# Quarter turn on the raw indices, one mask for sines and cosines, two standing index tiles

## The chip, the cores and the metric

The kernel runs on one core of a Trainium2 chip. The metric is device time in microseconds (us) of one execution, as the median of several runs. Five engines work side by side, each through its own instructions in order: TensorE (PE) multiplies matrices, VectorE (DVE) and ScalarE (ACT) do elementwise work, GpSimd (POOL) some small elementwise work, and SyncE (SP) issues all the transfers. An instruction that depends on another engine's result waits on a semaphore, and everything behind it on its own engine waits with it.

## The reference, cut to what matters

Audio of 32 rows is cut into 313 frames of 512 samples each, turned by a cosine transform, and passed through one attention layer and one feed-forward layer. The change touches only the feed-forward layer:

```python
wavelength = 1.0 + jnp.abs(W)                      # W is [256, 512]
theta = x[..., None, :] / wavelength + B_param     # x is [32, 313, 512], normalised
idx = jnp.mod(jnp.round(theta * (4096 / TWO_PI)), 4096).astype(jnp.int32)
sin_theta, cos_theta = sin_t[idx], cos_t[idx]      # tables of 4096 entries
cos_sum = jnp.sum(cos_theta * attn_cos, axis=-1)   # over the 512 features
sin_sum = jnp.sum(sin_theta * attn_sin, axis=-1)
out = einsum(cos_sum, proj_cos_w) + einsum(sin_sum, proj_sin_w)
return jax.nn.silu(out)
```

For each of 32 x 313 frames, 256 units and 512 features one index, one sine and one cosine are formed: 1.28 thousand million of each. The sums over the features are matrix products.

## The kernel before, in words

**Layout.** The 512 features lie on the 128 partitions in 4 chunks (`NC4`), the 313 frames of a sequence (`S`) along the free dimension. `xT` holds the normalised input of up to eight sequences, as a ring of four pairs. `f` holds, for each unit and feature, a factor and an offset, so that one VectorE instruction with an int16 output makes the rounded table index of one unit.

**Rounds and slots.** The 256 units are taken in 8 blocks of 32. A round (`ffn_round`, L566) does one block for all sequences that are in the ring; a pair joins at the round that `STARTS` gives and stays for eight rounds. The work of a round is cut into slots. A slot holds up to 16 (`SLOT`) stretches of 313 elements: `r` sequences times `n_p` combinations of unit and chunk. With two, four or eight sequences in the ring that is 5008 elements per partition, with six it is 3756.

**One slot before.** The steps are, with the lines of the profile:

1. L610 (`index`), VectorE: indices of the slot from `xT` and `f`, float32 to int16, in one instruction for every run of neighbouring pairs. It fills a new tile `ix`.
2. L622 (`mask`), VectorE: that tile in place, and 4095, exclusive or 2048. The second operation shifts the angle by half a turn, so that the sine's argument lies between -pi and pi.
3. L643 (`sines`), ScalarE: the sines of the tile, into a tile `trig`.
4. L630 (`quarter`), VectorE: the masked tile plus 1024 (a quarter turn), into a second tile `ix`.
5. L636 (`wrap`), VectorE: that second tile in place, and 4095.
6. L643 again, ScalarE: the sines of the second tile, which are the cosines.
7. L664 (`go`), TensorE: after each of the two activations, 16 (or 12) matrix products of `trig` with `hot`, which add into the PSUM banks `pa`.

In the code, the loop `for k in (1, 0)` goes through steps 1 to 3 with `k = 1` and through 4 to 6 with `k = 0`. There are four buffers `ix` (`N_IX`), so two slots' worth, and three buffers `trig`. A new tile of `ix` has to wait until the readers of the tile that lay in the buffer before it are done.

At the end of a round the banks are copied out (L681) and stored.

**What sets the order.** Nothing is issued as the code is walked through. Every step is added to a plan (`Plan`, with a key, an engine, an assumed duration, what it reads and what it writes). `Plan.emit` then plays the engines forward in time with these assumed durations and always takes, on each engine, the ready step with the lowest key. The order so found is the order of the instructions on each engine. The feed-forward rounds and the attention of later sequences (`attention`, with keys spread over the time that it may take) are thus woven into each other: attention's VectorE, ScalarE and TensorE instructions stand between those of the slots.

`swap` (L779) closes the buffers of the second sequence's attention and opens the pools in which `ix`, `trig`, `hot` and `f` lie. It comes before the first round.

Of the kernel before, what the change touches and what calls it, by code (L numbers as in the profile page):

```python
# [14 lines left out]
I16 = mybir.dt.int16  # L15
# [111 lines left out]
def tile_audio_tower(ctx: ExitStack, tc: tile.TileContext, t: dict, out: bass.AP):  # L127
# [5 lines left out]
    ROW0 = [i * STEP for i in range(NT)]  # L133
    NB = 4
    N_RING = 3
    N_IX, N_TRIG, N_HOT, N_PA = 4, 3, 2, 4

    const = ctx.enter_context(tc.tile_pool(name="const", bufs=1))
    psum = ctx.enter_context(tc.tile_pool(name="psum", bufs=1, space=PSUM))
# [426 lines left out]
    def ffn_round(plan, k0, blk, ring):  # L566

        pairs = [(at, pair) for at, pair in enumerate(ring) if pair is not None]  # L570
        r = 2 * len(pairs)
        runs = []
        for j, (at, _) in enumerate(pairs):
            if runs and runs[-1][0] + runs[-1][2] == at:
                runs[-1][2] += 1
            else:
                runs.append([at, j, 1])
        n_p = min(SLOT // r, 2 * NC4) if SLOT % r == 0 else 2
        E = n_p * r * S
        n_slots = 2 * NC4 // n_p  # L580
        n_banks = -(-r // 4)
        fz = place("f", 2)
        plan.add(k0 - 8, "SP", DMA_NS,
                 lambda: nc.sync.dma_start(
                     new("f", fz, [P, 2, NC4, UNITS], bufs=2), f_d[blk]),
                 ("f_d",), (("f", fz),))
        banks = {}
        key = k0
        for n in range(0, UNITS, 2):
            z = place("hot", N_HOT)  # L590
            plan.add(key - 4, "SP", DMA_NS,
                     lambda n=n, z=z: nc.sync.dma_start(
                         new("hot", z, [P, 2, NC4, 2, 32], bufs=N_HOT),
                         t["hot"][:, blk * UNITS + n : blk * UNITS + n + 2]),
                     (), (("hot", z),))
            todo = [(c, u) for c in range(NC4) for u in range(2)]
            for i in range(n_slots):
                parts = todo[i * n_p : (i + 1) * n_p]
                xs = None
                for k in (1, 0):  # L600
                    x = place("ix", N_IX)
                    if k == 1:
                        for pt, (c, u) in enumerate(parts):
                            for at, j, m in runs:
                                def index(x=x, pt=pt, c=c, u=u, n=n, at=at, j=j, m=m):
                                    if pt == 0 and j == 0:
                                        new("ix", x, [P, SLOT * S], I16, bufs=N_IX)
                                    d0 = (pt * r + 2 * j) * S
                                    f = now["f", fz]
                                    nc.vector.tensor_scalar(  # L610
                                        now["ix", x][:, d0 : d0 + 2 * m * S],
                                        now["xT", c][:, 2 * at * S : 2 * (at + m) * S],
                                        f[:, 0, c, n + u : n + u + 1], f[:, 1, c, n + u : n + u + 1],
                                        ALU.mult, ALU.add)
                                plan.add(key, "DVE", 233 + 0.521 * 2 * m * S, index,
                                         (("f", fz), *(("xT", c, at + y) for y in range(m))),
                                         (("ix", x),))


                        def mask(x=x):  # L620
                            tl = now["ix", x][:, :E]
                            nc.vector.tensor_scalar(  # L622
                                tl, tl, LUT - 1, LUT // 2, ALU.bitwise_and, ALU.bitwise_xor)
                        plan.add(key, "DVE", 130 + 0.26 * E, mask, (), (("ix", x),))
                        xs = x
                    else:

                        def quarter(x=x, xs=xs):
                            tl = new("ix", x, [P, SLOT * S], I16, bufs=N_IX)
                            nc.vector.tensor_scalar(  # L630
                                tl[:, :E], now["ix", xs][:, :E], float(LUT // 4), None, ALU.add)
                        plan.add(key, "DVE", 160 + 0.26 * E, quarter, (("ix", xs),), (("ix", x),))

                        def wrap(x=x):
                            tl = now["ix", x][:, :E]
                            nc.vector.tensor_scalar(tl, tl, LUT - 1, None, ALU.bitwise_and)  # L636
                        plan.add(key, "DVE", 130 + 0.26 * E, wrap, (), (("ix", x),))

                    w = place("trig", N_TRIG)

                    def sines(x=x, w=w):
                        tl = new("trig", w, [P, SLOT * S], bufs=N_TRIG)
                        nc.scalar.activation(tl[:, :E], now["ix", x][:, :E], AF.Sin,  # L643
                                             bias=-PI32, scale=ANG)
                    plan.add(key, "ACT", 110 + 0.8333 * E, sines, (("ix", x),), (("trig", w),))

                    first = n == 0 and i == 0
                    if first:  # L650
                        banks[k] = [place("pa", N_PA) for _ in range(n_banks)]

                    def go(k=k, n=n, w=w, z=z, parts=parts, first=first):
                        if first:
                            for p in banks[k]:
                                new("pa", p, [P, 512], bufs=N_PA, pool="bank")
                        for c in dict.fromkeys(c for c, _ in parts):
                            for bk, p in enumerate(banks[k]):
                                alone = r - 4 * bk == 2
                                for pt, (c_, u) in enumerate(parts):  # L660
                                    for b in range(min(4, r - 4 * bk) if c_ == c else 0):
                                        g = b + 2 * u if alone else b
                                        s0 = (pt * r + 4 * bk + b) * S
                                        nc.tensor.matmul(  # L664
                                            now["pa", p][g * 32 : g * 32 + 32, :S],
                                            now["hot", z][:, u, c, k, :],
                                            now["trig", w][:, s0 : s0 + S],
                                            start=(n == 0 and c == 0 and (alone or u == 0)),
                                            stop=(n == UNITS - 2 and c == NC4 - 1
                                                  and (alone or u == 1)),  # L670
                                        )
                    plan.add(key, "PE", 169 * n_p * r, go, (("trig", w), ("hot", z)),
                             [("pa", p) for p in banks[k]])
                    key += n_p * r / SLOT
                    if n < UNITS - 2 or i < n_slots - 1:
                        continue
                    m, r0 = blk * UNITS // P, blk * UNITS % P
                    for bk, p in enumerate(banks[k]):
                        u = place("part", 2)
                        plan.add(key, "DVE", 490,  # L680
                                 lambda u=u, p=p: nc.vector.tensor_copy(  # L681
                                     new("part", u, [P, S], bufs=2), now["pa", p][:, :S]),
                                 (("pa", p),), (("part", u),))
                        alone = r - 4 * bk == 2
                        for b in range(min(4, r - 4 * bk)):
                            sq = 2 * pairs[2 * bk + b // 2][1] + b % 2

                            which = [(b, 0, 1)] if not alone else [(b, 0, 2), (b + 2, 1, 2)]
                            for g, o, st in which:
                                plan.add(  # L690
                                    key, "SP", DMA_NS,
                                    lambda k=k, u=u, sq=sq, g=g, o=o, st=st: nc.sync.dma_start(
                                        sums_d[m, r0 + o : r0 + 32 : st, k, sq * S : (sq + 1) * S],
                                        now["part", u][g * 32 + o : g * 32 + 32 : st, :]),
                                    (("part", u),), (("sums_d", sq),),
                                )


    def load(key, *shape):
# [82 lines left out]
        pools["bank"] = ctx.enter_context(tc.tile_pool(name="bank", bufs=1, space=PSUM))  # L782
        for c in range(NC4):
            new("xT", c, [P, RING * S], bufs=NC4)
    plan.add(-9.0, "SP", 1, swap, (), [
        *plan.named("b"), *(("xT", c, at) for c in range(NC4) for at in range(RING // 2)),
        *(("hot", z) for z in range(N_HOT)), *(("f", z) for z in range(2))])


    life = NF // UNITS  # L790
# [10 lines left out]
                ring[at] = p  # L801
                joins[rd].append((p, at))
        rings.append(list(ring))
        key_of.append(key_of[-1] + 32.0 * sum(p is not None for p in ring))


    times, p, k = [], 1, 0.0
# [146 lines left out]
```

## Time and profile before

| | |
|---|---|
| median of 3 runs | 18893.47 us (18890.79 to 18904.49) |
| the profiled execution | 18894.1 us |
| its span | 18892.3 us |
| VectorE busy | 17770.2 us |
| ScalarE busy | 18090.3 us |
| TensorE matmul busy | 14803.3 us |
| mean granted TensorE clock | 0.926 |
| index (L610) | 5888 instructions, 6673.8 us |
| mask (L622), quarter (L630), wrap (L636) | 2144 each; 3023.7, 3014.4, 3017.3 us |
| sines (L643) | 4288 activations, 17547.6 us |

How to read it: the profile is of one execution. Busy time is time in which an engine worked on an instruction; where two instructions of an engine overlap, the time counts once. A group is all instructions of one line, operation and tile. What ended an engine's idle time is inferred from the semaphores. The page also cuts the span into 40 slices and gives each engine's busy share in tenths (9 is 90% or more); one slice is 472 us.

### The profile page before, as it was taken

What the parts mean: (1) busy time and instruction counts of PE and PEld (TensorE: products, weight loads), DVE (VectorE), ACT (ScalarE), POOL (GpSimd) and SP (SyncE); (2) the same over time, 40 slices, a digit from 0 to 9 for tenths busy, and PEclk for the clock granted to TensorE, in tenths of its full rate; (3) what the DMA queues carried; (4) which work ended last, traced back from release to release, by engine and by line L of the source; (5) the groups of instructions that cost most, each with busy time, mean ns of one, the idle gap of its engine ahead of it and who ended that gap; (6) DMA issues with size and microseconds to landing.
All of it is one profiled execution on the core that took longest, in us unless ns stands there. A gap on an engine that the chain in (4) does not pass through costs nothing.

```text
span 18892.3 us, 332980 instructions
## 1 busy us (share of the span) xinstructions
PE 14803.3 (78%) x148864; PEld 6590.0 (35%) x148864; DVE 17770.2 (94%) x15244; ACT 18090.3 (96%) x5026; POOL 656.5 (3%) x1222
## 2 busy tenths in 40 slices
PE   8888888887888887888788888887888788766566
PEld 4433333333333333333333333333333333222222
DVE  5999999999999999999999999999999999889998
ACT  3899999999999999999999999999999999999998
POOL 0000000000000000000000000000000000000000
PEclk8999999999999999999999999999999999889998
DMA  3211111111111111111111111111111111000011
GB/s 96 66 52 48 50 57 47 46 51 47 31 35 37 46 42 41 32 40 46 38 45 39 32 44 41 45 40 36 39 38 46 39 45 35 24 10 25 12 30 46
DMA packets 447834, 783.69 MB, mean 41 GB/s; under 512 B 61601, under 2 KB 116129, under 8 KB 446401
## 3 DMA queue, kind: packets, MB, share of 16 engines
q1 hardware_dynamic: 446400, 762.39, 13.3%
q8 instruction: 1167, 19.12, 0.4%
q14 instruction: 267, 2.18, 0.0%
HBM read 657.51 MB, written 104.66 MB: 40 GB/s over the span
## 4 chain that ended last, share of the span: by engine, by line
DVE 55%; ACT 18%; PE 15%; issue 8%; POOL 3%; DMA 1%; DVEq 0%; SPq 0%; ACTq 0%; POOLq 0%
DVE ix L610 20%; ACT trig L643 18%; DVE ix L630 9%; DVE ix L622 9%; PE pa L664 8%; DVE ix L636 8%; PE a_W L288 3%; PE a_W L273 2%; DVE a_mx L363 1%; DVE a_prob L372 1%; DVE a_sm L397 1%; DVE a_probT L424 1%; DVE a_st L236 1%; PE a_W L355 1%; POOL a_lu L224 1%
## 5 line engine op out<-in xcount | busy, mean ns | idle before, releaser
L643 ACT ACTIVATE trig<-ix 128x5008 f32<-128x5008 int16 (+1 forms) x4288 | 17547.6, 4178 | 442.0 <-PE pa L664 185.5
L664 PE MATMUL pa<-trig,hot 128*32 128x313 f32 x131072 | 10373.1, 462 | 3021.0 <-ACT trig L643 3003.0
L664 PEld LDWEIGHTS pa<-trig,hot 128*32 128x32 f32 x131072 | 4058.5, 116 | 8907.0 <-ACT trig L643 4513.9
L610 DVE TENSOR_SCALAR ix<-xT,f 128x2504 int16<-128x2504 f32 (+3 forms) x5888 | 6673.8, 1184 | 211.9 <-ACT trig L643 205.8
L630 DVE TENSOR_SCALAR ix<-ix 128x5008 int16<-128x5008 int16 (+1 forms) x2144 | 3014.4, 1406 | 201.2 <-DVE ix L622 5.0
L622 DVE TENSOR_SCALAR ix<-ix 128x5008 int16<-128x5008 int16 (+1 forms) x2144 | 3023.7, 1410 | 69.2
L636 DVE TENSOR_SCALAR ix<-ix 128x5008 int16<-128x5008 int16 (+1 forms) x2144 | 3017.3, 1407 | 67.2
L288 PE MATMUL a_W<-a_xnT,a_ring 128*128 128x313 f32 x4960 | 1539.2, 446 | 220.1 <-DVE a_u L341 125.1
L273 PE MATMUL a_W<-a_ring,a_u 128*105 128x512 f32 x2256 | 1101.5, 623 | 120.8 <-DVE a_u L499 53.7
L288 PEld LDWEIGHTS a_W<-a_xnT,a_ring 128*128 128x128 f32 x4960 | 882.9, 191 | 868.2 <-issue 284.7
L430 PE MATMUL a_W<-a_h,a_probT 105*105 105x64 f32 x4464 | 540.6, 270 | 118.0 <-DVE a_probT L424 117.7
L273 PEld LDWEIGHTS a_W<-a_ring,a_u 128*105 128x105 f32 x2256 | 360.2, 174 | 722.8 <-issue 579.0
L430 PEld LDWEIGHTS a_W<-a_h,a_probT 105*105 105x105 f32 x4464 | 476.3, 181 | 386.4 <-issue 194.7
L355 PE MATMUL a_W<-a_u 64*105 64x313 f32 x1488 | 502.8, 466 | 112.0 <-DVE a_prob L372 100.6
L412 PE MATMUL a_W<-ident,a_prob 105*105 105x105 f32 x2232 | 325.9, 284 | 186.7 <-ACT a_prob L384 150.9
L273 PE MATMUL a_W<-a_ring,a_xnT 128*105 128x512 f32 x744 | 380.0, 631 | 50.9 <-DVE a_xnT L210 49.3
L224 POOL TENSOR_TENSOR a_gu<-a_gr 105x24 f32<-105x24 f32 x93 | 69.5, 747 | 10066.3 <-DVE a_gr L218 10061.4
L412 PEld LDWEIGHTS a_W<-ident,a_prob 105*105 105x105 f32 x2232 | 259.4, 185 | 344.9 <-ACT a_prob L384 193.2
L260 PE MATMUL a_W<-ident,a_xn 105*128 105x105 f32 x1116 | 190.2, 298 | 234.8 <-DVE a_xn L248 108.2
L355 PEld LDWEIGHTS a_W<-a_u 64*105 64x105 f32 x1488 | 239.3, 178 | 386.0 <-DVE a_prob L372 152.6
L363 DVE TENSOR_REDUCE a_mx<-a_W 105x3 f32<-105x939 f32 x248 | 280.2, 1130 | 17.7 <-PE a_W L355 17.1
L424 DVE TENSOR_TENSOR a_probT<-a_W,a_dec 105x939 f32<-105x939 f32 x248 | 279.9, 1129 | 13.0 <-PE a_W L412 13.0
(136 smaller groups left out, 3461.9 us busy)
## 6 DMA issues: line engine op xcount, KB each, us to landing
hot<-in_hot SPq DMA_DIRECT2D x672, 256.0 KB
a_dec<-in_decay SPq DMA_DIRECT2D x248, 260.5 KB
a_ring<-in_proj SPq DMA_DIRECT2D x128, 256.0 KB
a_ring<-in_dct SPq DMA_DIRECT2D x124, 256.0 KB
a_ring<-wv_d SPq DMA_DIRECT2D x124, 256.0 KB
a_ring<-in_wq SPq DMA_DIRECT2D x124, 256.0 KB
a_ring<-in_wk SPq DMA_DIRECT2D x124, 256.0 KB
a_ring<-in_wq_s SPq DMA_DIRECT2D x124, 256.0 KB
```

Of the source, the lines that this page charges most:

```text
L273: lambda c=c, i=i, k=k, to=to: nc.tensor.matmul(x.W[:N, to, :], lhsT[:, c, ROW0[i] : ROW0[i] + N], x.ring[k], start=(c == 0), stop=(c == N ...
L288: lambda c=c: nc.tensor.matmul(x.W[:, bank, :S], w[:, c, :], x.xnT[:, c, :], start=(c == 0), stop=(c == NC4 - 1)),
L355: lambda i=i, qk=qk, r0=r0: nc.tensor.matmul(x.W[:N, i, :S], qk[r0 : r0 + DH, 0, ROW0[i] : ROW0[i] + N], qk[r0 : r0 + DH, 1, :], start=Tru ...
L363: lambda m=m: nc.vector.tensor_reduce(m[:N], x.W[:N, :NT, :S], AX.X, ALU.max),
L412: nc.tensor.transpose(x.W[:N, jj, ROW0[i] : ROW0[i] + N], x.prob[:N, a, i, ROW0[j] : ROW0[j] + N], ident[:N, :N],)
L430: nc.tensor.matmul(x.y[:N, i, (hd % 2) * DH : (hd % 2 + 1) * DH], x.probT[:N, jj, ROW0[i] : ROW0[i] + N], x.v[:N, jj, hd * DH : (hd + 1) * ...
L610: nc.vector.tensor_scalar(now["ix", x][:, d0 : d0 + 2 * m * S], now["xT", c][:, 2 * at * S : 2 * (at + m) * S], f[:, 0, c, n + u : n + u + ...
L622: nc.vector.tensor_scalar(tl, tl, LUT - 1, LUT // 2, ALU.bitwise_and, ALU.bitwise_xor)
L630: nc.vector.tensor_scalar(tl[:, :E], now["ix", xs][:, :E], float(LUT // 4), None, ALU.add)
L636: nc.vector.tensor_scalar(tl, tl, LUT - 1, None, ALU.bitwise_and)
L643: nc.scalar.activation(tl[:, :E], now["ix", x][:, :E], AF.Sin, bias=-PI32, scale=ANG)
L664: nc.tensor.matmul(now["pa", p][g * 32 : g * 32 + 32, :S], now["hot", z][:, u, c, k, :], now["trig", w][:, s0 : s0 + S], start=(n == 0 and ...
```

## The change

- A slot has one tile `ix` with two halves, in place of two tiles. The quarter turn (L619) is added to the raw indices of half 0 and goes into half 1; then one instruction (L624) masks both halves, with the and and the exclusive or that only the first tile had before. The separate wrap is gone.
- The first activation of a slot (L632) reads half 0 and the second half 1. Both read what the one mask has written.
- The tiles `ix` are no longer made anew in each slot: two of them (`N_IX` is 2) are made in `swap` and stay for the whole kernel.
- In the plan, quarter and mask have the key of the slot's first half; their assumed durations are set anew.
- The slots are made from one list over the round's units and chunks, in the same order as before, and `hot` is fetched at the first slot that needs it.

```diff
-    N_IX, N_TRIG, N_HOT, N_PA = 4, 3, 2, 4
+    N_IX, N_TRIG, N_HOT, N_PA = 2, 3, 2, 4
...
-        n_p = min(SLOT // r, 2 * NC4) if SLOT % r == 0 else 2
-        E = n_p * r * S
-        n_slots = 2 * NC4 // n_p
+        n_p = SLOT // r
...
+        todo = [(n + u, c) for n in range(0, UNITS, 2) for c in range(NC4) for u in range(2)]
+        slots = [todo[i : i + n_p] for i in range(0, len(todo), n_p)]
...
-                for k in (1, 0):
-                    x = place("ix", N_IX)
...
-                                    if pt == 0 and j == 0:
-                                        new("ix", x, [P, SLOT * S], I16, bufs=N_IX)
...
-                        def mask(x=x):
-                            tl = now["ix", x][:, :E]
-                            nc.vector.tensor_scalar(
-                                tl, tl, LUT - 1, LUT // 2, ALU.bitwise_and, ALU.bitwise_xor)
-                        plan.add(key, "DVE", 130 + 0.26 * E, mask, (), (("ix", x),))
...
-                        def quarter(x=x, xs=xs):
-                            tl = new("ix", x, [P, SLOT * S], I16, bufs=N_IX)
-                            nc.vector.tensor_scalar(
-                                tl[:, :E], now["ix", xs][:, :E], float(LUT // 4), None, ALU.add)
-                        plan.add(key, "DVE", 160 + 0.26 * E, quarter, (("ix", xs),), (("ix", x),))
-
-                        def wrap(x=x):
-                            tl = now["ix", x][:, :E]
-                            nc.vector.tensor_scalar(tl, tl, LUT - 1, None, ALU.bitwise_and)
-                        plan.add(key, "DVE", 130 + 0.26 * E, wrap, (), (("ix", x),))
...
+            x = place("ix", N_IX)
...
+                            now["ix", x][:, 0, d0 : d0 + 2 * m * S],
...
+            def quarter(x=x, E=E):
+                tl = now["ix", x]
+                nc.vector.tensor_scalar(tl[:, 1, :E], tl[:, 0, :E], float(LUT // 4), None, ALU.add)
+            plan.add(key, "DVE", 220 + 0.26 * E, quarter, (("ix", x, 0),), (("ix", x, 1),))
+
+            def mask(x=x, E=E):
+                tl = now["ix", x][:, :, :E]
+                nc.vector.tensor_scalar(
+                    tl, tl, LUT - 1, LUT // 2, ALU.bitwise_and, ALU.bitwise_xor)
+            plan.add(key, "DVE", 220 + 0.26 * 2 * E, mask, (), [("ix", x, i) for i in range(2)])
+            for k in (1, 0):
...
+                    nc.scalar.activation(tl[:, :E], now["ix", x][:, 1 - k, :E], AF.Sin,
+                                         bias=-PI32, scale=ANG)
+                plan.add(key, "ACT", 110 + 0.8333 * E, sines, (("ix", x, 1 - k),), (("trig", w),))
...
+        for x in range(N_IX):
+            new("ix", x, [P, 2, SLOT * S], I16, bufs=N_IX)
...
-        key_of.append(key_of[-1] + 32.0 * sum(p is not None for p in ring))
+        key_of.append(key_of[-1] + 512.0 / SLOT * sum(p is not None for p in ring))
```

## The prediction

> **What bounds the kernel now.** I read the page first: the busy totals, the forty slices, the chain that ended last.
>
> ```profile
> PE 14803.3 (78%) x148864; PEld 6590.0 (35%) x148864; DVE 17770.2 (94%) x15244; ACT 18090.3 (96%) x5026; POOL 656.5 (3%) x1222
> DVE  5999999999999999999999999999999999889998
> ACT  3899999999999999999999999999999999999998
> DVE 55%; ACT 18%; PE 15%; issue 8%; POOL 3%; DMA 1%; DVEq 0%; SPq 0%; ACTq 0%; POOLq 0%
> ```
>
> Two engines are full together. ScalarE (ACT) has 18892.3 - 18090.3 = 802 us without work in the whole span, so no saving on VectorE (DVE) can be worth more than that, while the chain runs mostly through VectorE. An average cannot settle which one sets the pace, so I cut the span into stages.
>
> ```profile
> core 0: us, PE busy (x) PEld busy (x) DVE busy (x) ACT busy (x) POOL busy (x), PEclk, DMA share, GB/s
> 325.00:1500.00 1175.00, 947.83 (x8906) 463.08 (x8907) 1108.91 (x1312) 1053.93 (x408) 62.72 (x126) 0.91 0.20 60
> 1500.00:3200.00 1700.00, 1392.90 (x13468) 650.30 (x13470) 1636.58 (x1555) 1589.42 (x443) 64.35 (x115) 0.93 0.16 50
> 3200.00:5000.00 1800.00, 1449.30 (x14204) 649.32 (x14200) 1715.45 (x1564) 1689.34 (x539) 78.82 (x152) 0.95 0.15 45
> 5000.00:15000.00 10000.00, 8067.52 (x81709) 3577.59 (x81698) 9563.56 (x7248) 9888.60 (x2531) 397.25 (x684) 0.93 0.13 40
> 16400.00:18500.00 2100.00, 1308.75 (x15640) 495.27 (x15632) 1960.45 (x1993) 2087.02 (x554) 0.00 (x0) 0.92 0.06 19
> ```
>
> The columns are the stretch, its length, then busy time by engine. From 325 to 5000 ACT lacks 121 + 111 + 111 = 343 us (7%); from 5000 to 18500 it lacks about 1%. So there are two regimes. After 5000 ScalarE is the bound: 111 us idle in 10000. Before 5000 something holds it up. The chain of waits (total us, times, longest), first for 1000 to 3000 us, then for the whole span, names it:
>
> ```profile
> ACT trig L643 <- DVE ix L622: 63.5, 48, 4.1
> ACT trig L643 <- PE pa L664: 35.2, 18, 5.2
> ACT trig L643 <- DVE ix L636: 24.2, 14, 2.8
> ```
>
> ```profile
> DVE ix L610 <- ACT trig L643: 205.8, 264, 2.7
> ```
>
> Early, the sines wait for the index tiles (L622, L636), while VectorE waits for ScalarE (L610, index tile not free) in that stretch for 2.9 us only; most of the 205.8 us lies late. VectorE is the early bound. One slot at the full ring in the timeline, the groups of one line by shape, and ScalarE's timeline near the end:
>
> ```profile
> 10017.78 3.07 DVE L610 TENSOR_SCALAR ix<-xT,f 128x2504 int16<-128x2504 f32 x2
> 10020.88 1.47 DVE L622 TENSOR_SCALAR ix<-ix 128x5008 int16<-128x5008 int16 x1
> 10022.45 1.47 DVE L630 TENSOR_SCALAR ix<-ix 128x5008 int16<-128x5008 int16 x1
> 10023.95 1.47 DVE L636 TENSOR_SCALAR ix<-ix 128x5008 int16<-128x5008 int16 x1
> 10025.34 3.07 DVE L610 TENSOR_SCALAR ix<-xT,f 128x2504 int16<-128x2504 f32 x2
> ```
>
> ```profile
> L636 DVE TENSOR_SCALAR ix<-ix 128x5008 int16<-128x5008 int16 x1760 | 2578.2, 1465 | 55.4
> L636 DVE TENSOR_SCALAR ix<-ix 128x3756 int16<-128x3756 int16 x384 | 439.1, 1143 | 11.8
> ```
>
> ```profile
> 18698.37 150.01 ACT L643 ACTIVATE trig<-ix 128x5008 f32<-128x5008 int16 x35
> ```
>
> From start to start a VectorE slot takes 3.10 + 1.57 + 1.50 + 1.39 = 7.56 us; ScalarE's two sines take 2 x 150.01 / 35 = 8.57 us. Attention's VectorE work is put between: 2041 us (17770 less the four groups' 15,729), nearly all of it before 16400.
>
> **What the Trainium skill says.** "VectorE: DVE Perf Modes", in "The TRN2 errata", has a fixed cost per SBUF instruction, measured near 150 cycles, beside the cost per element. The trace agrees: (1465 - 1143) / (5008 - 3756) = 0.257 ns per element, leaving 177 ns fixed. The same page, in "What auto-detection actually checks", gives 16-bit one-source operations in SBUF four elements a cycle when the outermost count is even or equal; 0.257 ns is that rate at the page's 0.96 GHz, but no row of before has two separate rows. "ScalarE: Activation LUTs", in "What ACT_TABLE_LOAD costs", says that back-to-back activations overlap by about 93 ns; here each sine shows 4365 ns and the next starts 4286 ns after it, 79 ns of overlap.
>
> **The change part by part.**
>
> Removed: two masks a slot (L622 and L636, 2144 each), together 6041 us of busy time. Added: one mask over both halves. Its estimate: 1465 + 5008 x 0.257 = 2754 ns, and 1143 + 3756 x 0.257 = 2110 ns for the six-sequence rounds. 1760 x 2.754 + 384 x 2.110 = 5657 us. Busy time falls by 384 us, 0.18 us a slot. The quarter add stays one instruction of the same size. With the gaps: after is index 3.10, quarter 1.50 to 1.57, mask 1.39 + 1.29 = 2.68, so 7.28 to 7.35 us against 7.56. I take 0.21 us a slot (end 0.28); at 3756 elements the starts (1.25, 1.18, 1.05) give the same. 2144 x 0.21 = 450 us of VectorE's time, 2.5%.
>
> What of it counts: from 325 to 5000 there are 1101 sines, 550 slots: 550 x 0.21 = 116 us, if VectorE alone sets the pace. It doesn't wholly. ScalarE also waits there for TensorE (PE), 128 us in all, when matmuls on trig stand behind attention's matmuls, and VectorE itself waits for POOL and PE for some 110 us, both of which stay as long. I take 70%: 80 us; ends 40 and 116. From 5000 to 18500 the saving falls behind ScalarE, which covers it: 13500 us hold about 1550 slots, 326 us of saved work, but ScalarE's waits for index tiles there are only 30 us and for TensorE 57. I take 15 us; ends -60 and +80. If ScalarE's cover were gone it would be 326.
>
> Moved: the first sine. Before, it waited for index and mask, 3.10 + 1.47 = 4.6 us of a slot; in the built order of the changed kernel both sines stand behind the one mask, after the quarter add. Buffer reuse is unchanged: index waits for the first sine of two slots earlier, the quarter add for the second, in both kernels, so the standing tiles hold the same two slots as the four old tiles. From the time that the index tile is free, three sines of 4.29 (12.86 us) go by before the first sine is needed. Before, 4.6 us of VectorE's work had to fit in, leaving 8.3 us for attention's instructions; now 3.10 + 1.5 + 2.75 = 7.4 us, leaving 5.5. The waiting sine holds back only what is behind it on ScalarE, then the matmuls on TensorE, and attention's matmuls queued behind those. In the orders of both programs, the slots that hold more than 5.5 us of attention (instructions by their rows' means) are 17 before and 5 after of 2144, and those over 4 us 105 and 95. So I cost it at nothing where VectorE has its lead, and at the -60 end where it has not. At the start, once: first sine at 331.0, now 3 us later, in a stretch where VectorE is the bound, so hidden.
>
> Edits with one answer, nothing: the slot list, `key_of` and the loads of hot (same sizes: SLOT is 16 and divides as before); no DMA, no matmul and no activation is added. The last 150 us are one unbroken run of sines.
>
> Sum against the profiled execution (18894.1 us, span 18892.3, 0.6 us above the median of 18893.47): 18894 - 80 - 15 = 18799. I predict 18800 us.
>
> **The rivals.**
>
> *ScalarE is the bound throughout* (13%). For: 96% busy. Against: 7% idle before 5000, and the waits on L622. Then the early saving turns into longer waits of L610 for the sines and of ACT for PE: 10 to 35 us gained, about 18875.
>
> *The late stage gives too* (14%). ScalarE's remaining waits after 5000, 87 us, come partly from attention work late on VectorE; if two thirds go (58) and the early stage gives all 116: about 18715.
>
> *The first sine comes too late* (13%, the other side). Place: score phases after 5000, where two instructions of 1.13 to 1.15 us per head (L363, L372) fall into successive slots. A slot then takes 7.35 + 2.3 = 9.65 us against 8.57 and VectorE loses 1.1 us of its lead per slot, so a full lead of 5.5 us lasts five such slots; before, 1.3 us from 8.3, over six slots. It decides where more than five follow one another or the lead was not full. Of the attention passes, 20 come after 5000 us; at 7 us lost in each it is 140 us: 18894 - 80 + 140 = 18954. It cancels the early gain at 4 us a pass. Against: the late waits on L622 were 2.5 us in all, and 0.21 us more lead is won per slot.
>
> *The mask does not keep its rate* (4%) when its halves are not adjacent, which is so for the 384 slots of 3756 elements (at 5008 the built program has one run of 10016). At half the rate: 384 x 7512 x 0.257 ns = 740 us more, two thirds of it early where VectorE is the bound: 18894 - 80 + 493, about 19300. The change then would not do what it says.
>
> **How the numbers follow.** The likeliest case (56%): 18740 to 18856, at 18800. About 0.2% (38 us) is what a measurement of this kernel can tell from no change. Faster: 56 + 14 = 70%. Same: 13%. Slower: 13 + 4 = 17%. The range 18685 to 18920 takes in the first three cases but for the ends, and leaves out the 17% above and some 3% below.
>
> **What would show it.** The mask's group near 2754 and 2110 ns, x2144; the quarter add still 1465; VectorE's busy time near 17390; ScalarE's busy time unchanged at 18090 (each step's sizes). ScalarE's idle time from the start to the end of the early rounds down by 40 to 116 us, in waits for L622's successor; later, the index instructions waiting for sines well over 205.8 us in all, which is where the covered saving goes. Wrong if ScalarE's waits for the mask after 5000 exceed 100 us (first sine too late), if the two-row mask takes over 3 us, or if the saved early time comes back as waits for TensorE.

## The result and the profile after

The changed kernel takes 18832.92 us (median of 7 runs, 18820.34 to 18839.53) against 18896.91 us (7 runs): a ratio of 0.9965, 95% interval 0.9954 to 0.9977. That is 64 us saved where 94 were forecast, and inside the range. The profiled execution took 18838.41 us, its span 18836.6.

From the page of the kernel after, the busy totals and the chain that ended last by engine:

```profile
PE 14740.8 (78%) x148864; PEld 6575.9 (35%) x148864; DVE 17450.4 (93%) x13100; ACT 18081.3 (96%) x5026; POOL 722.1 (4%) x1222
ACT 31%; DVE 30%; PE 24%; issue 11%; POOL 3%; DMA 1%; SPq 0%; ACTq 0%; DVEq 0%; POOLq 0%
```

VectorE has 2144 instructions fewer and is busy for 320 us less (384 were forecast); ScalarE does the same work. The chain, 55% VectorE before, is now shared out. The groups by shape (count, busy us, mean ns, idle before, its releaser):

```profile
L624 DVE TENSOR_SCALAR ix<-ix 128x10016 int16<-128x10016 int16 x1760 | 4872.8, 2769 | 54.6
L619 DVE TENSOR_SCALAR ix<-ix 128x5008 int16<-128x5008 int16 x1760 | 2579.2, 1465 | 576.9 <-ACT trig L632 472.4 <-DVE ix L607 1.8
L624 DVE TENSOR_SCALAR ix<-ix 128x7512 int16<-128x7512 int16 x384 | 814.1, 2120 | 11.8
```

The mask is at its price: 2769 and 2120 ns, where 2754 and 2110 had been worked out. So the two halves that do not touch, in the 384 slots of 3756 elements, keep the rate of one run, as the Trainium skill has it for an even outermost count ("VectorE: DVE Perf Modes", "What auto-detection actually checks"). Unlooked-for is the second line: the quarter add waits for ScalarE, 472 us in this shape.

One slot in the timeline, start first:

```profile
10014.72 3.07 DVE L607 TENSOR_SCALAR ix<-xT,f 128x2504 int16<-128x2504 f32 x2
10017.89 1.47 DVE L619 TENSOR_SCALAR ix<-ix 128x5008 int16<-128x5008 int16 x1
10019.39 2.77 DVE L624 TENSOR_SCALAR ix<-ix 128x10016 int16<-128x10016 int16 x1
10022.08 1.13 DVE L424 TENSOR_TENSOR a_probT<-a_W,a_dec 105x939 f32<-105x939 f32 x1
```

From start to start that is 3.17 + 1.50 + 2.69 = 7.36 us, against 7.56 before: 0.20 us a slot. Over the whole traces, the slots of 5008 elements with no wait and no other work between have the same medians, 7.36 and 7.56. Over 2144 slots it is 429 us of VectorE's time, of which 64 arrived. The same stages as before (stretch, length, busy time by engine):

```profile
325.00:1500.00 1175.00, 948.50 (x8908) 462.89 (x8908) 1094.91 (x1202) 1052.18 (x408) 69.44 (x126) 0.91 0.20 60
1500.00:3200.00 1700.00, 1385.21 (x13613) 650.70 (x13615) 1626.67 (x1381) 1607.03 (x449) 76.90 (x128) 0.94 0.17 50
3200.00:5000.00 1800.00, 1455.51 (x14348) 656.75 (x14341) 1702.65 (x1329) 1710.48 (x548) 84.56 (x139) 0.95 0.15 45
5000.00:15000.00 10000.00, 8058.80 (x81850) 3578.86 (x81846) 9411.48 (x6129) 9893.63 (x2527) 435.92 (x684) 0.94 0.13 40
```

ScalarE's idle time from 325 to 5000 us fell from 342 to 305 us, 37 us; from 5000 to 15000 it fell by 5, after 15000 by 5 again, and its work is 9 us shorter. That makes the 56 us between the two spans. So early only about half of what was forecast came. The early waits of ScalarE are not those that I had named. From 325 to 5000 us (total us, times, longest), first before, then after:

```profile
ACT trig L643 <- PE pa L664: 127.7, 52, 6.1
ACT trig L643 <- DVE ix L622: 123.2, 78, 8.8
ACT trig L643 <- DVE ix L636: 42.2, 23, 2.8
ACT trig L643 <- issue: 37.2, 12, 6.2
```

```profile
ACT trig L632 <- DVE ix L624: 168.4, 78, 11.6
ACT trig L632 <- PE pa L654: 119.5, 64, 6.7
ACT trig L632 <- issue: 4.4, 1, 4.4
```

The waits for masks, which were to fall, went from 165 to 168 us. The gain lies in the waits for TensorE, which were to stay (8 us less), and in those marked "issue", for which the profile shows no releaser (33 us less); what those waited for stays open. Over the whole run, first before, then after:

```profile
ACT trig L643 <- DVE ix L622: 126.8, 89, 8.8
...
ACT trig L643 <- DVE ix L636: 69.6, 50, 2.8
```

```profile
DVE ix L619 <- ACT trig L632: 541.8, 684, 3.5
...
ACT trig L632 <- DVE ix L624: 253.5, 130, 11.6
...
ACT trig L632 <- PE pa L654: 138.1, 85, 6.7
```

Before, ScalarE waited 126.8 + 69.6 = 196 us for masks and wraps; now 254 us for the mask, though VectorE does less. From 5000 to 18500 us these waits rose from 30 to 84 us, while those for TensorE fell from 57 to 16. VectorE and ScalarE each wait for the other more than before: a sign that what lies ready between them has become less.

### The profile page after: what moved, and what is told of

Read it like the earlier page. It is cut to its first block, busy times and chain, and to the rows that moved or that the text cites. A ratio compares the mean times of both kernels' runs of the same rounds, so it can differ in the third digit from the quotient of the medians.

```text
span 18836.6 us, 330714 instructions
## 1 busy us (share of the span) xinstructions
PE 14740.8 (78%) x148864; PEld 6575.9 (35%) x148864; DVE 17450.4 (93%) x13100; ACT 18081.3 (96%) x5026; POOL 722.1 (4%) x1222
## 4 chain that ended last, share of the span: by engine, by line
ACT 31%; DVE 30%; PE 24%; issue 11%; POOL 3%; DMA 1%; SPq 0%; ACTq 0%; DVEq 0%; POOLq 0%
ACT trig L632 30%; PE pa L654 16%; DVE ix L607 10%; DVE ix L624 9%; DVE ix L619 5%; PE a_W L288 3%; PE a_W L273 3%; DVE a_mx L363 1%; POOL a_lu L225 1%; POOL a_lu L224 1%; PE a_W L355 1%; DVE a_prob L372 1%; POOL a_lu L226 0%; ACT a_prob L384 0%; DVE a_st L236 0%
## 5 line engine op out<-in xcount | busy, mean ns | idle before, releaser
L632 ACT ACTIVATE trig<-ix 128x5008 f32<-128x5008 int16 (+1 forms) x4288 | 17538.8, 4178 | 401.5 <-DVE ix L624 253.5
L624 DVE TENSOR_SCALAR ix<-ix 128x10016 int16<-128x10016 int16 (+1 forms) x2144 | 5686.9, 2652 | 66.4
L619 DVE TENSOR_SCALAR ix<-ix 128x5008 int16<-128x5008 int16 (+1 forms) x2144 | 3017.5, 1407 | 667.8 <-ACT trig L632 541.8
L224 POOL TENSOR_TENSOR a_lu<-a_lr 105x3 f32<-105x3 f32 x186 | 106.4, 572 | 4072.8 <-DVE a_lr L218 4063.1
```

The lines of the kernel that those rows point to most:

```text
L224: nc.gpsimd.tensor_tensor(u, r, r, ALU.mult)
L619: nc.vector.tensor_scalar(tl[:, 1, :E], tl[:, 0, :E], float(LUT // 4), None, ALU.add)
L624: nc.vector.tensor_scalar(tl, tl, LUT - 1, LUT // 2, ALU.bitwise_and, ALU.bitwise_xor)
L632: nc.scalar.activation(tl[:, :E], now["ix", x][:, 1 - k, :E], AF.Sin, bias=-PI32, scale=ANG)
```

## The lead, worked out again

"Lead" here is the time that VectorE may spend on attention's work in one slot before ScalarE runs dry, when it is as far ahead as the tiles let it be. In the built order the index of a slot waits for the first sine of two slots earlier, the quarter add for the second sine of two slots earlier. Before, that second wait came after index and mask, 4.6 us into the slot, when the second sine (4.29 us) was over. Now it comes after the index alone, at 3.2 us, so a VectorE that is fully ahead stands still until 4.29. The mask then ends at 4.29 + 1.50 + 2.77 = 8.6 us and the first sine is due at 12.9: a lead of 4.3 us, not 5.5. Before it was 8.3.

*Theory 1*: the time is set by VectorE's slot and by this lead together; the change earns with the first and pays with the second. *Theory 2*: the lead costs nothing; the rest of the gain is held up by TensorE's waits and attention's chains. Two further questions: what in the change shortens the slot, and how much of the 64 us is chance in the order of instructions, since each kernel gets its own from the planner. All times below are also given as a difference to the kernel before, measured beside each; the intervals on these ratios reach some 25 us to either side.

## Experiments

**Two masks again, half 1 first** (`split_late`).

```diff
-            def mask(x=x, E=E):
-                tl = now["ix", x][:, :, :E]
+            for h in (1, 0):
+                def mask(x=x, E=E, h=h):
+                    tl = now["ix", x][:, h, :E]
...
+                plan.add(key, "DVE", 110 + 0.26 * E, mask, (("ix", x, 1),) if h == 0 else (), [("ix", x, h)])
...
-                plan.add(key, "ACT", 110 + 0.8333 * E, sines, (("ix", x, 1 - k),), (("trig", w),))
+                plan.add(key, "ACT", 110 + 0.8333 * E, sines, [("ix", x, i) for i in range(2)], (("trig", w),))
```

> Standing tiles and the quarter turn on raw indices as in the change, but two masks again, half 1 first and half 0 last, so both sines still wait for the whole slot. VectorE has four instructions a slot as before the change (7.56 us). Theory 1, the change pays for its shorter VectorE slot with a smaller lead of the first sine (4.3 us instead of 8.3): slower than before, 18920 to 18990 us, ScalarE's waits for masks over 300 us. Theory 2, the lead costs nothing and only VectorE's instruction counts: within 20 us of before, 18880 to 18915.

Measured: 19166.71 us, +269 us, ratio 1.0142 (1.0128 to 1.0155). That is more than theory 1 had, and the test was not clean: with the last line the planner takes half 0 as in use until the second sine, and puts attention's VectorE work ahead of the index: counted in the traces, some 1710 us of it stand right behind a mask and 290 us behind an index, where `split_early` (next) has some 1030 and 990. ScalarE waits 601 us for masks. So the run mixes the lead with another order and doesn't decide between the theories; it shows only how much the order around the index can cost.

**The same, half 0 first** (`split_early`): `for h in (0, 1)`, without the two added conditions in the plan.

> The same with half 0 masked first, so that the first sine needs one mask fewer. VectorE's work as in split_late. Theory 1: 20 to 60 us faster than split_late, about 18900 to 18940. Theory 2: the same as split_late within 15 us.

Measured: 18838.88 us, -58 us, ratio 0.9969 (0.9958 to 0.9981): as fast as the change, with the same number of instructions a slot as before it. This I had not expected. The timeline of `split_early`:

```profile
10010.46 3.07 DVE L607 TENSOR_SCALAR ix<-xT,f 128x2504 int16<-128x2504 f32 x2
10013.70 1.47 DVE L619 TENSOR_SCALAR ix<-ix 128x5008 int16<-128x5008 int16 x1 [0.17 <-ACT trig L633]
10015.20 2.84 DVE L625 TENSOR_SCALAR ix<-ix 128x5008 int16<-128x5008 int16 x2
10017.96 3.08 DVE L607 TENSOR_SCALAR ix<-xT,f 128x2504 int16<-128x2504 f32 x2
```

The two masks take 2.84 us together although each shows 1.47: the second starts 1.37 us after the first. From the first to the next slot's index it is 2.76 us, against 2.69 with the one mask. So merging the masks saves 0.07 us a slot. The other 0.13 us come from the raw quarter turn: before, each of mask, quarter and wrap waited for the instruction in front of it (quarter and wrap started 1.57 and 1.50 us after it); now the quarter add and the first mask do, and the second mask waits for neither. VectorE's busy time bears it out: 17565.9 us here against 17770.2 with the same number of instructions, the overlap of the pair (0.10 us a slot).

**The clean version of the late order** (`split_late2`): `split_early` with half 1 masked first, and a token in the plan that keeps the two sines in their order and does nothing else.

```diff
-            for h in (0, 1):
+            for h in (1, 0):
...
-                plan.add(key, "DVE", 110 + 0.26 * E, mask, (), [("ix", x, h)])
+                plan.add(key, "DVE", 110 + 0.26 * E, mask, (("ix", x, 1),) if h == 0 else (),
+                         [("ix", x, h)] + ([("masked", x)] if h == 0 else []))
...
-                plan.add(key, "ACT", 110 + 0.8333 * E, sines, (("ix", x, 1 - k),), (("trig", w),))
+                plan.add(key, "ACT", 110 + 0.8333 * E, sines, (("ix", x, 1 - k), ("masked", x)), (("trig", w),))
```

> As split_early but half 1 masked first, with the planner told of nothing else than that both sines come after the mask of half 0 (in split_late it was also told that half 0 stays in use until the second sine, which moved attention's work). VectorE's slot 7.43 us as in split_early, the lead of the first sine 12.9 - 4.3 - 4.3 = 4.3 us instead of 5.6. Theory 1, the lead prices the change: 20 to 100 us slower than split_early, 18860 to 18940. Theory 2, it does not, and split_late was slow through the order alone: within 15 us of split_early, 18825 to 18855.

Measured: 18896.26 us, -5 us, ratio 0.9998 (0.9990 to 1.0007). VectorE is busy for 17565.7 us, as in `split_early` to 0.2 us, and attention's work stands much as it stood (some 1080 us behind masks, 990 behind indices). The first sine is released one mask later, 1.4 us, and the run is 53 us longer. In ScalarE's busy time, 15 us of the loss lie before 5000 us and 35 between 5000 and 15000. In the waits, first `split_early`, then `split_late2`:

```profile
DVE ix L619 <- ACT trig L633: 459.5, 607, 3.5
...
ACT trig L633 <- DVE ix L625: 211.3, 147, 10.3
...
ACT trig L633 <- issue: 40.0, 17, 4.5
```

```profile
ACT trig L634 <- DVE ix L625: 314.3, 165, 11.7
...
ACT trig L634 <- issue: 4.4, 1, 4.4
```

ScalarE's waits for masks went up by 103 us, those with no releaser shown down by 36. That is outside what theory 2 forecast. But the two orders are not the same: of the 2924 VectorE instructions outside the slots' own rows, 2273 stand in the same slot in both, the others one slot off. So part of the 53 us can be order; further down, another order alone makes 20 to 35 us. Against the kernel before, `split_late2` has a slot 0.13 us shorter and a lead 4.0 us shorter, and takes the same time. The change differs from `split_late2` in the merged mask (and its own order): it has the same lead, 4.3 us, and is 59 us faster for 0.07 us x 2144 = 150 us less of VectorE's time.

**Fresh tiles** (`split_early_fresh`): four tiles of one half each, made anew, in place of the two standing ones.

```diff
-            x = place("ix", N_IX)
+            x = (place("ix", N_IX), place("ix", N_IX))
...
-                tl = now["ix", x]
-                nc.vector.tensor_scalar(tl[:, 1, :E], tl[:, 0, :E], float(LUT // 4), None, ALU.add)
+                tl = new("ix", x[1], [P, SLOT * S], I16, bufs=N_IX)
+                nc.vector.tensor_scalar(tl[:, :E], now["ix", x[0]][:, :E], float(LUT // 4), None, ALU.add)
```

> split_early with four tiles made anew, one for each half, in place of the two standing ones. It differs from the kernel before in one thing: the quarter turn is added to the raw indices, so that the instructions after it do not each wait for the one in front. If the standing tiles are worth nothing: 18825 to 18855, as split_early. If they carry the gain: 18880 to 18910, as before.

Measured: 18838.71 us, -63 us, ratio 0.9968 (0.9956 to 0.9981). Here the order is the same as in `split_early` (all 2924 VectorE instructions outside the slots' rows stand in the same slot), so the pair is clean: the standing tiles are worth nothing; they are needed only so that one mask can span both halves. And the raw quarter turn without merged mask or standing tiles brings as much as the whole change. More than the one thing named above sets it apart from the kernel before, though: the first sine now waits for the quarter add too, and the assumed costs, and with them the order, are others.

**The planner's assumed cost** (`plan_costs`, `split_early_costs`, `before_costs`): one number in the plan each.

```diff
-            plan.add(key, "DVE", 220 + 0.26 * 2 * E, mask, ...)
+            plan.add(key, "DVE", 80 + 0.26 * 2 * E, mask, ...)
```

> The changed kernel with one number altered: the planner's assumed duration of the mask, 80 + 0.26 x 2E ns instead of 220 + 0.26 x 2E, near the 2.69 us from start to start that was measured. Only the order of instructions can change. If the order was tuned by the assumed cost: 10 to 30 us either way, 18805 to 18860. If not: the same as the change within 10 us.

> split_early with the planner's assumed mask 40 + 0.26E ns instead of 110 + 0.26E. If a lower assumed cost gives a better order as in plan_costs: 18800 to 18825. If that was chance: 18830 to 18860.

> The kernel before with the assumed costs of mask and wrap 60 + 0.26E ns instead of 130 + 0.26E, nothing else. If the order found with lower assumed costs is worth 20 us by itself: 18865 to 18885. If the order only pays once VectorE's slot is really shorter: 18890 to 18920.

Measured: `plan_costs` 18810.77 us, 22 us below the change (-87; ratio 0.9954, 0.9940 to 0.9968); `split_early_costs` 18819.16 us, 20 us below `split_early` (-83; 0.9958, 0.9946 to 0.9971); `before_costs` 18935.68 us, +34 us (1.0018, 1.0010 to 1.0026), beyond what I had for it. In each of the three pairs the two kernels' times do not overlap, so the order alone is worth 20 to 35 us either way. It is not a matter of assuming the true cost: the change's slot was assumed at 3076 + 1522 + 2824 ns = 7.42 us and measured at 7.36, and 140 ns less (7.28) is no nearer. Both kernels with the raw quarter turn gained by the lower figure, and the one before lost. Why is left open; what the runs settle is that differences of this size between kernels with different orders prove nothing by themselves.

**No quarter turn** (`no_quarter`): the quarter add and the mask of half 1 are left out and both sines read half 0.

> The quarter add and the mask of half 1 are left out; both sines read half 0, so the cosines are not computed. VectorE's slot falls to about 4.6 us and its lead is large. Theory 1, VectorE's pace and lead are what is left: ScalarE alone bounds it, its 18081 us of work plus 330 us before the first sine, 45 at the end and some waits for TensorE: 18480 to 18600. Theory 2, what is left are waits for TensorE and attention's chains that VectorE doesn't govern: 18700 or more.

Measured: 18566.72 us, -331 us, ratio 0.9825 (0.9811 to 0.9838). With a VectorE that is only 64% busy, ScalarE's waits for masks are 20 us:

```profile
DVE ix L607 <- ACT trig L627: 5475.7, 1879, 6.9
...
ACT trig L627 <- PE pa L649: 135.5, 76, 5.6
ACT trig L627 <- DVE ix L619: 20.3, 12, 8.8
```

ScalarE's own work is 18060 us here, so this is near the floor that it sets for this layout. VectorE's pace and lead together thus held about 330 us in the kernel before (to within the 35 us that another order can make), of which the change takes 64; of the waits for TensorE, 135 us remain even here.

**The lead in steps** (`slot8_ix2`, `slot8_ix3`, `slot8_ix4`): the changed kernel with `SLOT = 8` and two, three and four standing tiles; tiles of half the size leave room for more of them. All fixed costs come twice as often, so these three are compared with each other.

> The changed kernel with slots of 8 stretches instead of 16, two standing tiles. Everything is issued in halves, so fixed costs double: ScalarE's sine takes about 2.2 us, VectorE's slot about 3.9 us. The lead is three sines less one sine, quarter and mask: 6.6 - 4.5 = about 2.1 us. Theory 1: ScalarE waits for masks over 700 us, over 19700 us. Theory 2: set by ScalarE's work alone (18081 + 4288 x 0.1 = about 18500 busy), 19250 to 19400.

> As slot8_ix2 with three standing tiles: lead five sines less 4.5 us, about 6.5 us. Theory 1: 200 us or more faster than slot8_ix2. Theory 2: the same within 30 us.

> As slot8_ix2 with four standing tiles: lead seven sines less 4.5 us, about 11 us. Theory 1: faster still than slot8_ix3, by 30 us or more, with ScalarE's waits for masks under 200 us. Theory 2: the same as slot8_ix3.

Measured: 20006.28, 19681.29 and 19625.82 us (ratios to before 1.0582, 1.0411 and 1.0381, each within 0.0017). ScalarE's waits for masks:

```profile
ACT trig L632 <- DVE ix L624: 712.2, 428, 10.4
```

```profile
ACT trig L632 <- DVE ix L624: 396.0, 206, 10.6
```

```profile
ACT trig L632 <- DVE ix L624: 293.9, 147, 8.2
```

From a lead of 2.1 to 6.5 us the time falls by 325 us, from 6.5 to 11 by another 55, the second not far above what another order can make. The direction is theory 1's; that the waits with four tiles would be under 200 us was wrong. The kernels of slot 16 have leads of 4 to 10 us, where this curve still falls.

**More lead at full slot size** (`five_halves`): `split_early_fresh` with a fifth half tile. The room comes from attention's buffers.

```diff
-    N_RING = 3
-    N_IX, N_TRIG, N_HOT, N_PA = 4, 3, 2, 4
+    N_RING = 2
+    N_IX, N_TRIG, N_HOT, N_PA = 5, 3, 2, 4
...
-            self.dec = [sb(f"dec{i}", STEP * (NT - 1) + S) for i in range(2)]
+            self.dec = [sb("dec0", STEP * (NT - 1) + S)] * 2
...
-                plan.add(key, "DVE", 110 + 0.26 * E, mask, (), [("ix", x[h])])
+                plan.add(key, "DVE", 40 + 0.26 * E, mask, (), [("ix", x[h])])
```

> split_early_fresh with five half tiles instead of four (the room for the fifth comes from attention: two weight buffers instead of three, one decay buffer instead of two) and the planner's mask at 40 + 0.26E ns. The quarter add now waits for a sine that ends one sine earlier, so the lead of the first sine grows from 5.6 to about 9.9 us. Lead theory: ScalarE's waits for masks fall from some 210 us to under 150, and the time to 18730 to 18790 against 18819 for the same costs with four. If the lead no longer matters beyond 5.6 us: waits as in split_early and 18810 to 18830. If attention's smaller buffers cost more than the lead brings: above 18840, with new waits of TensorE for DMA.

Measured: 18703.55 us, -199 us, ratio 0.9897 (0.9881 to 0.9914): the fastest of all, and 116 us below `split_early_costs`, which differs in the fifth half, attention's buffers and the order. It is also below the 18730 us that I had for the lead at best. ScalarE's waits for masks in `split_early_costs`, then the waits of `five_halves`:

```profile
ACT trig L633 <- DVE ix L625: 161.4, 97, 10.3
```

```profile
DVE ix L621 <- ACT trig L635: 332.4, 447, 1.7
```

```profile
ACT trig L635 <- PE pa L657: 126.7, 58, 8.2
ACT trig L635 <- DVE ix L627: 112.5, 55, 8.5
```

```profile
325.00:5000.00 4675.00, 3811.39 (x37023) 1790.39 (x37027) 4478.25 (x4480) 4385.66 (x1408) 214.88 (x393) 0.93 0.18 51
5000.00:15000.00 10000.00, 8109.00 (x82684) 3607.34 (x82677) 9555.51 (x7327) 9990.49 (x2557) 420.94 (x684) 0.94 0.14 40
```

ScalarE's waits for masks are 112 us (161 with four halves), and in the late stage it is busy for 9990 of 10000 us; before, 9889. The smaller attention buffers cost little: TensorE's matmuls wait for `a_ring` for 20 us in all, 17 before, and its weight loads for 21 us, 5 before. Part of the gain over the four halves may be order; 116 us is well beyond the 20 to 35 us found above, but no run has the smaller buffers without the fifth half.

## Why the prediction was right, and where its terms were off

*Price of the mask and of the slot*: right. 2754 and 2110 ns forecast, 2769 and 2120 measured; 0.21 us a slot forecast, 0.20 measured. But the reason given, one fixed cost fewer, is only a third of it: of the 177 ns that I had as the fixed part, all but 0.07 us is overlapped where an instruction waits for nothing in front of it, and merging is worth that 0.07 us. The other 0.13 us came from an edit that I had costed at nothing, the quarter turn on raw indices, which takes one wait out of the row. VectorE's busy time came to 17450 us where 17390 was the sign: 30 us of this are the mask's own groups (5687 us for 5657); the rest is not traced. One reading was slightly off: 150.01 us are 34 steps and one whole sine, so a sine starts 4284 ns after the last and overlaps it by 81, not 4286 and 79.

*"I take 70%: 80 us; ends 40 and 116"*: this term was mis-sized, and reached by another way than the one named. The early stage gave 37 us, and not in waits for masks, which rose by 3 us, but in waits for TensorE, which I had as unchanged, and in waits with no releaser shown. (The 1101 sines counted for the term are 1093 in the trace, which changes it by less than 1 us.)

*"I take 15 us"* for the late stage: 19 came (5 and 5 us of idle time and 9 us less work), in part by luck. I had ScalarE's late waits as they were; in fact those for masks rose by 54 us and those for TensorE fell by 41. Two changes that I had not foreseen nearly cancelled.

*"I cost it at nothing where VectorE has its lead"*: this is the step that failed, although the late sum came out. I had 5.5 us of lead left after the move of the first sine and called it enough, from a count of slots with more attention work than that. The lead was 4.3 us, because "buffer reuse is unchanged" holds for which sine is waited for, not for when: the quarter add's wait moved up to a point where it still bites, and L619 waited 541.8 us. And a burst need not use up the whole lead to cost something: VectorE is seldom fully ahead (the quarter add waited for a sine in 684 of 2144 slots). One mask's time of lead, 1.4 us, went with 53 us of run time in that pair, 35 of them between 5000 and 15000 us. The lead lost against the kernel before is 4.0 us, so I take it to have eaten a good part of what the shorter slot earned; no run has the change's slot with the old lead, so how much is not measured. That is the third rival, "the first sine comes too late", at work inside the likeliest case: its waits after 5000 us came to 84 us, short of the 100 that I had named as the sign.

*The sign that index instructions would wait well over 205.8 us for sines*: wrong place. The index waits 18 us, the quarter add 542.

*ScalarE the bound throughout*: some 330 us of the run were held up by VectorE, as `no_quarter` shows, so this rival was rightly put low.

What stays open: how the 64 us divide between shorter slot, lost lead and order, since another order alone makes 20 to 35 us; what the early waits with no releaser shown were; and whether `five_halves` gains from anything but its lead.

## What to carry to other kernels

Where two engines are both near full, look not only at each engine's time per piece but at how far ahead the producer may run: for every result ask how much of the producer's work lies between the buffer coming free and the result being released, and where in that row each wait for a buffer stands. An instruction less in the row can cost as much lead as it saves time; one more buffer can be worth more than either (116 us here against 64, with an order of its own).

Before an instruction is merged away to save its fixed cost, see from start to start what it really costs in the row. If it does not wait for its neighbour, most of the fixed cost may already be hidden.

## What the runs showed of the hardware

Two masks on VectorE of 1465 ns each that don't depend on each other start 1.37 us apart (`split_early`); where the second instruction waits for the first the distance is 1.50 us, and 1.57 where it also waits for ScalarE (with that wait long since met; both in the kernel before). The Trainium skill, in "VectorE: DVE Perf Modes", "The DRAIN you can't avoid", has eight copies in a row taking the same time with a semaphore after each and with one after the last only, so that the semaphore cost nothing extra there; here the wait on the engine's own semaphore goes with 0.13 us, read from the timelines of three kernels, and for these instructions the measurement decides. No run separates it from the dependence itself.

A mask over two rows of 3756 int16 elements that do not touch took 2120 ns, against 1143 ns for one row and 2769 ns for 10016 elements in one run: each element more costs 0.260 ns in both.
